# Collecting the states of a selective scan four units at a time instead of three

## The chip, the cores and the metric

The kernel runs on one NeuronCore of a Trainium2 chip. The metric is the device time of one execution in microseconds (us). Before the change it is 14725.35 us, the median of three runs (14713.78 to 14727.14). Engines are called as in the profile: PE is the matrix engine (PEld its weight loads), DVE the vector engine, ACT the scalar engine, POOL the GpSimd engine, SP the engine whose queue issues almost all DMAs.

## The reference

Four images of 96 channels and 64 x 64 points (L = 4096 points) pass through four layers: an attention layer, a two-dimensional selective scan with a convolutional block behind it (L1), a sharpening convolution (L2), and a second selective-scan layer (L3). The scan is what matters here. For each image it runs in four directions (rows and columns, forward and back) over 192 channels, each with 16 states:

```
h = h * exp(d * A) + (d * u) * B          # 16 states of every channel, point after point
y = sum over the 16 states of h * C       # one number per channel and point
Y = y_rows + y_rows_back + y_cols + y_cols_back + u * D
```

The sum over the 16 states in the second line is the part that the change regroups.

## The kernel before

**Units.** The eight scans (two layers, four images) make eight stages of 384 units, 3072 units in all. A unit is 8 channels x 16 states = 128 partitions, over a chunk of CH = 1024 points. Twelve units (NG) are a group: 96 channels (one half h of the 192), one direction, one chunk. There are 256 groups. The order of instructions in the loop is written out by hand, in `unit` (line 2036). For unit i it issues, in this order:

- on SP, `fetch(i+4)` (line 1936): the step sizes d of the unit's 8 channels are read from DRAM and repeated for 16 states, into one of 10 buffers `rep`; then the store of a finished y chunk, if there is one, and DMAs that were put off (`later`);
- on ACT, `decays(i+2)` (line 1943, shown in the profile at L1948): exp(d A), in place in `rep`;
- on DVE, `scan(i)` (L1969): the recurrence, into `hs`; then on ACT `carry_on` (L1977), which keeps the last state;
- on POOL, `times_c(i)` (L1981): hs * C, written back into the unit's `rep` buffer;
- on PE, where due, `collect(j)` (line 1983, PE instructions are all at L948): the sum over 16 states, as matmuls of `rep` with a 0/1 matrix `addn`, accumulated in the PSUM tile `acc`;
- on PE, `drive(i+2)` (line 1950): (d u) spread from `parts` over the 128 partitions into one of two PSUM tiles `bx`; it needs the buffer that `scan(i)` has read;
- on DVE, `times_b(i+1)` (L1962): bx * B, in place.

**Collecting three at a time.** PE can be split into column tiles of 32 columns, each with its own weights and its own moving operand. `place` (line 1930) hands out the channels so that three units in a row belong to three different column tiles: unit m of the group holds channels of column tile m % 3. A collect takes three units and is due when (i - 4) is a multiple of 3. One group has four collects; in the first, `acc` is started (and the chunk of y that a backward direction adds to is loaded into `yo`), after the last `output` (line 2000) writes `yo` from rows 0 to 95 of `acc`, and a DMA (L2017) stores it to a y image in DRAM. There is one `yo` buffer and one `acc`.

**Work beside the scan.** The other layers are generators (`first`, `second`, `third`, `last`, with `directions` and `finish` in them). Each `yield` hands control back to the scan loop. In stages 0, 3 and 4 the attention layer and its convolutions (`first`) of another image run beside the scan, in stages 1, 2, 5 and 6 the block behind the L1 scan (`second`), in stage 7 the rest of L3 for all four images. How much of it is issued in a unit is set by a budget, counted in matmuls:

```
PACE = {"first": 3.5, "second": 3.7, "third": 3.2}
owed = min(owed, 0.5) + PACE[...] - (2.1 if i % 3 == 1 else 0.0)
```

so a unit with a collect gives the work beside it 2.1 less. At most two pieces go into one unit. What is left of it 19 units before a stage's end is issued at once. `prepare(g)` (line 1835), also beside the scan, makes d, B, C and d u of the group after next.

**y images.** `directions` (line 1418) begins `second` and `third`: once the scan's last chunks are stored, it loads the row and column images of y for both halves h, in chunks of 96 x 1024 (L1430 and L1432), 8 DMAs for each half, with SP in between waiting for the last store. `last` and `finish` load y images too.

## Time and profile before

| | |
|---|---|
| median of three runs | 14725.35 us |
| span of the profiled execution | 14698.9 us |
| what lies around the span (median less span) | 26.5 us |
| first scan begins, last scan begins | 690.3 us, 14567.0 us |
| 3072 scans, DVE (L1969) | 7156.4 us busy, about 2.33 us each |
| 3072 products with B, DVE (L1962) | 3723.6 us busy, 1.21 us each |
| 1024 collects on PE (`acc`) | 2586.7 us busy |
| bytes moved by DMA | 2644.27 MB |
| mean granted PE clock | 0.817 |

The execution's own time was not recorded apart from its span, so the difference to the median of the runs stands in for start and end. A matmul with float32 operands appears as two weight loads and two MATMUL records, so a collect of six matmuls is twelve records. The distance from one scan to the next, here called the pitch, is the loop's time per unit; it is read from the records of L1969. Divided over sixteenths of a stage (24 units) it runs like this, in us:

| sixteenth | 1 | 2 | 3 | 4 | 5 | 6 | 7 | 8 | 9 | 10 | 11 | 12 | 13 | 14 | 15 | 16 |
|---|---|---|---|---|---|---|---|---|---|---|---|---|---|---|---|---|
| stage 0 (`first`) | 4.75 | 5.02 | 4.88 | 4.94 | 4.97 | 4.72 | 4.66 | 4.85 | 4.14 | 4.08 | 3.87 | 3.82 | 4.08 | 4.31 | 3.98 | 3.92 |
| stage 1 (`second`) | 5.99 | 5.31 | 4.04 | 3.99 | 3.94 | 4.06 | 4.27 | 4.48 | 4.03 | 4.80 | 4.92 | 3.75 | 4.09 | 4.27 | 3.75 | 3.96 |
| stage 7 (`third`, `last`) | 5.70 | 5.90 | 4.51 | 4.23 | 6.52 | 5.75 | 4.93 | 4.23 | 6.57 | 6.05 | 5.21 | 4.66 | 5.09 | 5.36 | 5.24 | 5.10 |

A stage is 1671 to 1730 us long, stage 7 is 2036 us.

### The profile page before, as it was taken

Reading aid. Unit: us, or ns where it says so; the run is one execution under the profiler, and the core shown is the slowest. Engines: PE = TensorE matmul, PEld = TensorE weight load, DVE = VectorE, ACT = ScalarE, POOL = GpSimd, SP = SyncE. Lnnn points to the kernel's source line nnn. Section 1 sums busy time; section 2 is a strip of 40 time slices with the busy share of each in tenths; the row PEclk is TensorE's granted clock in tenths of the full one; section 3 lists DMA queues with packets and bytes.
Section 4 is the critical chain, followed back from the end, with each engine's and each line's share of the span. In section 5 each row is a group of like instructions: output and inputs, shape, how many; then the busy total and the mean of one; then the engine's idle time right before and its main releaser. Section 6 shows DMA issues by size and latency. Waiting matters only on the chain.

```text
span 14698.9 us, 128101 instructions
## 1 busy us (share of the span) xinstructions
PE 12296.5 (84%) x40802; PEld 3348.5 (23%) x40802; DVE 11654.4 (79%) x7509; ACT 8721.7 (59%) x12340; POOL 10204.0 (69%) x4634
## 2 busy tenths in 40 slices
PE   8888987988889796889868887897979888777767
PEld 2322221222223121222212222222212222111111
DVE  0477888888878888778887888788888888778776
ACT  3355565556756666554755556566755567666554
POOL 0166787777868778667776788687777777666564
PEclk9878887988879787778867887897979888677666
DMA  0266787787878778667876778687787878776674
GB/s 9 72 158 163 188 212 198 188 204 184 221 175 200 197 199 209 154 166 193 211 189 160 178 200 220 172 205 189 203 200 189 204 190 215 175 181 169 165 182 108
DMA packets 902735, 2644.27 MB, mean 180 GB/s; under 512 B 107104, under 2 KB 257216, under 8 KB 902048
## 3 DMA queue, kind: packets, MB, share of 16 engines
q1 hardware_dynamic: 901392, 2634.72, 71.8%
q8 instruction: 324, 5.31, 0.2%
q14 instruction: 363, 2.97, 0.1%
q10 hardware_dynamic: 656, 1.27, 0.0%
HBM read 2168.97 MB, written 466.62 MB: 179 GB/s over the span
## 4 chain that ended last, share of the span: by engine, by line
PE 50%; DVE 20%; ACT 10%; DMA 7%; issue 6%; POOL 5%; SPq 1%; DVEq 0%; POOLq 0%; ACTq 0%
PE one L948 33%; DVE hs L1969 14%; PE acc L948 9%; PE bx L948 6%; DVE bx L1962 5%; DMA rep<-dd 3%; PE held L948 3%; POOL rep L1981 2%; ACT rep L1948 2%; ACT L1948 1%; ACT ex L1287 1%; ACT L1890 1%; DMA xz<-gate 0%; ACT delta L1888 0%; POOL delta L1893 0%
## 5 line engine op out<-in xcount | busy, mean ns | idle before, releaser
L1981 POOL TENSOR_TENSOR rep<-hs,bc 128x1024 f32<-128x1024 f32 x3072 | 7224.5, 2357 | 3210.5 <-DVE hs L1969 2664.2
L1969 DVE TENSOR_TENSOR_SCAN hs<-rep,carry,bx 128x1024 f32<-128x1024 f32 x2304 | 5401.7, 2344 | 274.0 <-POOL rep L1981 14.8
L1962 DVE TENSOR_TENSOR bx<-bx,bc 128x1024 f32<-128x1024 f32 x3072 | 3723.6, 1212 | 1086.2 <-PE bx L948 1063.5
L1948 ACT ACTIVATE rep<-rep,l_decay 128x1024 f32<-128x1024 f32 x3072 | 3495.7, 1143 | 513.3 <-DMA rep<-dd 493.8
L948 PE MATMUL bx<-parts,spread 24*128 24x512 bf16 x6144 | 1412.7, 435 | 1662.7 <-DVE hs L1969 1608.8
L948 PE MATMUL acc<-rep,ct 128*32 128x512 f32 x12288 | 2586.7, 741 | 9.8 <-POOL rep L1981 9.1
L1969 DVE TENSOR_TENSOR_SCAN hs<-rep,bx 128x1024 f32<-128x1024 f32 x768 | 1754.7, 2285 | 123.3 <-ACT carry L1977 29.0
L948 PEld LDWEIGHTS <-spread 24*128 24x128 bf16 x6144 | 310.4, 93 | 4154.6 <-DVE hs L1969 2755.2
L948 PE MATMUL one<-band,dg 96*96 96x512 f32 x2304 | 1075.9, 605 | 0.0
L948 PE MATMUL one<-upad,diag 96*96 96x512 f32 x2016 | 996.4, 632 | 0.0
L948 PE MATMUL one<-qq,kk 96*128 96x512 f32 x1152 | 818.8, 800 | 134.6 <-ACT ex L1287 84.0
L948 PEld LDWEIGHTS acc<-rep,ct 128*32 128x32 f32 x12288 | 506.2, 127 | 1742.4 <-issue 1494.2
L1287 ACT ACTIVATE ex<-one 128x512 f32<-128x512 f32 x576 | 343.1, 596 | 747.7 <-PE one L948 743.0
L948 PE MATMUL one<-pr,ct 6*96 6x512 f32 x1024 | 652.7, 728 | 84.3 <-DVE V L1192 10.4
L1948 ACT ACT_TABLE_LOAD x495 | 635.1, 1283 | 76.6 <-DMA rep<-dd 68.5
L948 PE MATMUL one<-hp,diag 96*96 96x512 f32 x1152 | 607.1, 668 | 28.6 <-POOL diag L1112 28.6
L948 PE MATMUL one<-vpad,diag 96*96 96x512 f32 x1200 | 611.7, 647 | 0.0
L1977 ACT COPY carry<-hs 128x1 f32<-128x1 f32 x2304 | 409.2, 178 | 308.4 <-DVE hs L1969 306.5
L948 PE MATMUL held<-ex,cols 128*32 128x256 f32 x3072 | 567.9, 450 | 7.9 <-ACT ex L1287 1.9
L948 PE MATMUL held<-ex,vT 128*32 128x256 f32 x3072 | 568.3, 451 | 0.0
L948 PEld LDWEIGHTS one<-band,dg 96*96 96x96 f32 x2304 | 346.6, 162 | 535.3 <-issue 516.8
L948 PEld LDWEIGHTS one<-upad,diag 96*96 96x96 f32 x2016 | 314.7, 169 | 489.2 <-issue 478.3
(3420 smaller groups left out, 14369.3 us busy)
## 6 DMA issues: line engine op xcount, KB each, us to landing
rep<-dd SPq DMA_DIRECT2D x3072, 512.0 KB
parts<-du SPq DMA_DIRECT2D x1024, 144.0 KB
bc<-rows SPq DMA_DIRECT2D x256, 512.0 KB
dd<-delta SPq DMA_DIRECT2D x256, 384.0 KB
du<-cut SPq DMA_DIRECT2D x256, 384.0 KB
us<-urow SPq DMA_DIRECT2D x128, 384.0 KB
du<-cut SPq DMA_DIRECT2D x256, 192.0 KB
yrow<-yo SPq DMA_DIRECT2D x128, 384.0 KB
```

What stands on the lines that cost most here:

```text
L948: nc.tensor.matmul(o, lhsT=lhsT, rhs=rhs, start=first, stop=last)
L1287: nc.scalar.activation(last.rearrange("p a b -> p (a b)"), p, AF.Exp, scale=HD**-0.5)
L1890: nc.scalar.activation(w, w, AF.Ln)
L1948: nc.scalar.activation(a, a, AF.Exp, scale=decay[tag][:, k, NG * h + m : NG * h + m + 1])
L1962: nc.vector.tensor_mul(bx, bx, ready[i // NG][2][:, 0, :])
L1969: nc.vector.tensor_tensor_scan(out=hs, data0=a, data1=bx, initial=carry[:, h, m : m + 1] if c else 0.0, op0=ALU.mult, op1=ALU.add)
L1977: nc.scalar.copy(carry[:, h, m : m + 1], live[i][1][:, CH - 1 : CH])
L1981: nc.gpsimd.tensor_tensor(a, hs, ready[i // NG][2][:, 1, :], ALU.mult)
```

## The change

Units are handed out over four column tiles in place of three, so that a collect takes four units and a group has three collects. Each column tile then holds 24 channels in 32 rows; rows 24 to 31 of each are zero. `acc` and `yo` and the y images in DRAM have 128 rows with these gaps. Whoever loads a y image into a tile of 96 rows does it in four DMAs of 24 rows (`ungapped`) where it was one of 96; the first chunk of an L3 row scan likewise loads u into `yo` in four. `yo` becomes one tile that lives through the kernel and is cleared once. The sums of D come from a new constant of 128 rows. There are 12 buffers `rep` in place of 10, and the space that the framework sets aside for descriptors of DMAs issued by POOL is cut to 1024 bytes (this kernel issues none there). The budget takes 2.1 off in every fourth unit, where it was every third. The collect follows its last unit at the same distance as before (`i - 5` with four units, `i - 4` with three), and the output comes in the same unit of the group.

```
-            dsum[tag] = derived(2)
-            nc.vector.tensor_reduce(dsum[tag], wv(tag + "d"), AX.X, ALU.add)
+            dsum[tag] = keep.tile([128, 2], F32, name=tag + "dsum")
+            nc.vector.tensor_reduce(dsum[tag], cv("d")[:, 0 if tag == "l1_" else 1], AX.X, ALU.add)
...
+    y_row, y_col = ([image(f"{k}{h}_", 128) for h in range(2)] for k in ("yrow", "ycol"))
+
+    def ungapped(dst, src, cols):
+
+        for q in range(4):
+            nc.sync.dma_start(out=dst[24 * q : 24 * q + 24], in_=src[32 * q : 32 * q + 24, cols])
...
                 for j in range(4):
-                    nc.sync.dma_start(out=t.rearrange("p a b -> p (a b)")[:, bass.ts(j, CH)],
-                                      in_=y_col[h][b][:, bass.ts(j, CH)])
-                    nc.sync.dma_start(out=V[:, h, bass.ts(j, CH)], in_=y_row[h][b][:, bass.ts(j, CH)])
+                    ungapped(t.rearrange("p a b -> p (a b)")[:, bass.ts(j, CH)], y_col[h][b], bass.ts(j, CH))
+                    ungapped(V[:, h, bass.ts(j, CH)], y_row[h][b], bass.ts(j, CH))
...
-        return g, m % 3 * 4 + m // 3
+        return g, m % 4 * 3 + m // 4
...
-        rep = sp.tile([128, CH], F32, name="rep", bufs=10)
+        rep = sp.tile([128, CH], F32, name="rep", bufs=12)
...
-        hs = [live.pop(i + q)[0] for q in range(3)]
-        w = addn[:, 24 - 8 * (m // 3) : 56 - 8 * (m // 3)]
+        hs = [live.pop(i + q)[0] for q in range(4)]
+        w = addn[:, 24 - 8 * (m // 4) : 56 - 8 * (m // 4)]
         for e in range(2):
-            for q in range(3):
-                mm(live["acc"][bass.ts(q, 32), bass.ts(e, PCH)], w, hs[q][:, bass.ts(e, PCH)], m == 0, m == NG - 3)
+            for q in range(4):
+                mm(live["acc"][bass.ts(q, 32), bass.ts(e, PCH)], w, hs[q][:, bass.ts(e, PCH)], m == 0, m == NG - 4)
...
-        j = i - BEHIND - 2
-        due = j >= 0 and j % 3 == 0
+        j = i - BEHIND - 3
+        due = j >= 0 and j % 4 == 0
...
-            owed = min(owed, 0.5) + PACE[BESIDE[s][0][0]] - (2.1 if i % 3 == 1 else 0.0)
+            owed = min(owed, 0.5) + PACE[BESIDE[s][0][0]] - (2.1 if i % 4 == 1 else 0.0)
...
-    nc = bacc.Bacc("TRN2", target_bir_lowering=False, num_devices=1)
+    nc = bacc.Bacc("TRN2", target_bir_lowering=False, num_devices=1,
+                   dynamic_dma_scratch_size=1024)
```

More of the change, by code (lines that the diff above doesn't have):

```diff
@@ L172, in _constants @@
     c["dtw2"] = s.reshape(128, 4, E)
+    s = np.zeros((4, 32, 2, 2, 4), np.float32)
+    for t, w in enumerate((i["L1_conv_Ds"], i["L3_conv_ss_D"])):
+        s[:, :24, t] = w.reshape(4, 2, 4, 24).transpose(2, 3, 1, 0)
+    c["d"] = s.reshape(128, 2, 2, 4)
     for tag, w in (("l1_", i["L1_conv_A_log"]), ("l3_", i["L3_conv_ss_Alog"])):
@@ L1024, in streams, with image @@
             nc.vector.tensor_scalar(decay[tag], src, -1.0, None, ALU.mult)
-            dsum[tag] = derived(2)
-            nc.vector.tensor_reduce(dsum[tag], wv(tag + "d"), AX.X, ALU.add)
-    def image(name):
-        return [dram.tile([96, L], F32, name=f"{name}{b}") for b in range(B)]
+            dsum[tag] = keep.tile([128, 2], F32, name=tag + "dsum")
+            nc.vector.tensor_reduce(dsum[tag], cv("d")[:, 0 if tag == "l1_" else 1], AX.X, ALU.add)
+    def image(name, rows=96):
+        return [dram.tile([rows, L], F32, name=f"{name}{b}") for b in range(B)]
     res1, res2, gate1, skip3, gate3 = (image(k) for k in ("res1_", "res2_", "gate1_", "skip3_", "gate3_"))
-    u_row, u_col, y_row, y_col = ([image(f"{k}{h}_") for h in range(2)] for k in ("urow", "ucol", "yrow", "ycol"))
+    u_row, u_col = ([image(f"{k}{h}_") for h in range(2)] for k in ("urow", "ucol"))
+    y_row, y_col = ([image(f"{k}{h}_", 128) for h in range(2)] for k in ("yrow", "ycol"))
+    def ungapped(dst, src, cols):
+        for q in range(4):
+            nc.sync.dma_start(out=dst[24 * q : 24 * q + 24], in_=src[32 * q : 32 * q + 24, cols])
     def group_norm(src, dst):
@@ L1643, in last @@
                     for j in range(4):
-                        nc.sync.dma_start(out=t.rearrange("p a b -> p (a b)")[:, bass.ts(j, CH)],
-                                          in_=y_col[h][b][:, bass.ts(j, CH)])
+                        ungapped(t.rearrange("p a b -> p (a b)")[:, bass.ts(j, CH)], y_col[h][b], bass.ts(j, CH))
                     yield 1
@@ L1683, in load @@
                     t = pool.tile([96, PCH], F32, tag=name, name=name, bufs=bufs)
-                    nc.sync.dma_start(out=t, in_=src[b][:, bass.ts(j, PCH)])
+                    if src[b].shape[0] == 128:
+                        ungapped(t, src[b], bass.ts(j, PCH))
+                    else:
+                        nc.sync.dma_start(out=t, in_=src[b][:, bass.ts(j, PCH)])
                     return t
@@ L1811, in streams @@
     carry = keep.tile([128, 2, NG], F32, name="carry")
+    yo = keep.tile([128, CH], F32, name="yo")
+    nc.gpsimd.memset(yo, 0.0)
     sums = keep.tile([96, len(SCANS), 4, 2, 2 * NCH], F32, name="sums")
@@ L1988, in collect @@
             live["acc"] = ps.tile([128, CH], F32, tag="acc", name="acc", bufs=1)
-            live["yo"] = sp.tile([96, CH], F32, name="yo", bufs=1)
             if back:
-                nc.sync.dma_start(out=live["yo"], in_=(y_row if axis == "r" else y_col)[h][b][:, natural(c, back)])
+                nc.sync.dma_start(out=yo, in_=(y_row if axis == "r" else y_col)[h][b][:, natural(c, back)])
             elif axis == "r" and tag == "l3_":
-                nc.sync.dma_start(out=live["yo"], in_=u_row[h][b][:, natural(c, back)])
-        hs = [live.pop(i + q)[0] for q in range(3)]
-        w = addn[:, 24 - 8 * (m // 3) : 56 - 8 * (m // 3)]
+                for q in range(4):
+                    nc.sync.dma_start(out=yo[32 * q : 32 * q + 24],
+                                      in_=u_row[h][b][24 * q : 24 * q + 24, natural(c, back)])
+        hs = [live.pop(i + q)[0] for q in range(4)]
+        w = addn[:, 24 - 8 * (m // 4) : 56 - 8 * (m // 4)]
         for e in range(2):
-            for q in range(3):
-                mm(live["acc"][bass.ts(q, 32), bass.ts(e, PCH)], w, hs[q][:, bass.ts(e, PCH)], m == 0, m == NG - 3)
+            for q in range(4):
+                mm(live["acc"][bass.ts(q, 32), bass.ts(e, PCH)], w, hs[q][:, bass.ts(e, PCH)], m == 0, m == NG - 4)
     def output(i):
@@ L2004, in output @@
         dst = (y_row if axis == "r" else y_col)[h][b][:, natural(c, back)]
-        yo = live["yo"]
-        ya = time(live["acc"][:96], back, 0, CH)
+        ya = time(live["acc"], back, 0, CH)
         if back:
@@ L2065, in unit @@
             times_b(i + 1)
-        if due and j % NG == NG - 3:
+        if due and j % NG == NG - 4:
             store.append(output(j))
@@ L2142, in streams @@
                 work.run()
-            owed = min(owed, 0.5) + PACE[BESIDE[s][0][0]] - (2.1 if i % 3 == 1 else 0.0)
+            owed = min(owed, 0.5) + PACE[BESIDE[s][0][0]] - (2.1 if i % 4 == 1 else 0.0)
             owed = unit(i, prep, work, owed)
-        for j in range(total - 3, total, 3):
+        for j in range(total - 4, total, 4):
             collect(j)
```

## The prediction

> **What bounds the kernel now.** I read the page's busy times first, then the pitch over sixteenths of a stage, then three windows, and last who makes DVE wait.

> ```profile
> PE 12296.5 (84%) x40802; PEld 3348.5 (23%) x40802; DVE 11654.4 (79%) x7509; ACT 8721.7 (59%) x12340; POOL 10204.0 (69%) x4634
> ...
> L948 PE MATMUL acc<-rep,ct 128*32 128x512 f32 x12288 | 2586.7, 741 | 9.8 <-POOL rep L1981 9.1
> ```

> PE is busiest, but no engine is full. The windows say why (columns: us, busy PE, PEld, DVE, ACT, POOL, then PE clock, DMA share, GB/s). First attention in stage 0, second the convolutions of stage 1, third the end of stage 0, where nothing but scan and `prepare` is left:

> ```profile
> 1116.00:1329.00 213.00, 192.13 (x919) 48.43 (x918) 159.24 (x97) 119.16 (x184) 143.35 (x63) 0.79 0.67 167
> 2664.00:2950.00 286.00, 285.62 (x918) 86.68 (x916) 251.22 (x145) 176.58 (x252) 234.38 (x102) 0.99 0.80 198
> 2299.00:2393.00 94.00, 46.14 (x160) 8.28 (x160) 85.32 (x51) 48.79 (x53) 77.97 (x35) 0.61 0.89 216
> ```

> In the convolutions PE is full at full clock (285.62 of 286), with a pitch of 4.0 us. In attention it is 90% busy at clock 0.79 and waits on exponentials in between; pitch 4.9. Where no work is beside the scan, DVE is 91% busy, and the pitch, 3.9, comes close to scan and product (2.33 + 1.21 = 3.54). So a stage is a stretch at PE's pace and a tail at DVE's. The waits of DVE agree: the scan loop's large wait is for PE's `drive`.

> ```profile
> DVE bx L1962 <- PE bx L948: 1063.5, 485, 27.1
> ...
> DVE yo L2008 <- PE acc L948: 190.6, 84, 9.2
> ```

> At each start of `second` there is a third regime, where SP's queue decides. In order of time, stage 1:

> ```profile
> 2408.72 2.29 DVE L1969 TENSOR_TENSOR_SCAN hs<-rep,bx 128x1024 f32<-128x1024 f32 x1
> ...
> 2411.30 0.31 SPq L1430 DMA_DIRECT2D yc<-ycol  x1
> 2411.66 0.42 SPq L1432 DMA_DIRECT2D V<-yrow  x1
> ...
> 2415.51 0.52 SPq L1940 DMA_DIRECT2D rep<-dd  x1
> ...
> 2429.72 1.15 ACT L1948 ACTIVATE rep<-rep,l_decay 128x1024 f32<-128x1024 f32 x1 [3.87 <-DMA rep<-dd]
> ```

> Eight y loads of 384 KB go out in 4.2 us, and the `rep` fetch behind them lands 18.4 us after the first. The scans around it start at 2412.26, 2422.85 and 2431.04: about 12 us lost.

> [...] the three tiles of a collect start within 14 ns of each other, at 2402.393, and the next three 0.852 us later, what one untiled matmul part takes at the same half clock; attention already runs four such tiles side by side at the same rate. [...] The trace's clock records are only 0.5 and 1.0; hence a collect of 1.85 us at full clock and 3.16 us or more at half. [...]

> **The change part by part.**

> *Collects.* 1024 become 768; a collect of four tiles should take what one of three takes. The mean is 2586.7 / 1024 = 2.53 us, so PE is freed of 256 x 2.53 = 647 us. Beside work it is less, at a higher clock: 31.59 us for 14 collects in the attention window (2.26 each), 46.83 for 24 in the convolutions (1.95). Per unit a collect costs 0.75 and 0.65 us there, and would cost 0.56 and 0.49: 0.19 and 0.16 freed, say 0.18.

> *Budget.* It rises from 3.5 - 0.7 = 2.8 to 3.5 - 0.525 = 2.975 in `first`. So PE's freed time is filled with more work per unit, and that work ends earlier. I took the end from the two programs' instruction orders: the last PE instruction beside the scan falls in unit 353 before and 335 after (stages 0, 3, 4), 349 and 331 (stages 1, 2, 5, 6). In each of seven stages 18 units move from the busy stretch (pitch about 4.4 over 350 units) to the tail (3.9). With n busy units, side work S, other cost c per busy unit on the path and tail pitch f, a stage takes S + n c + (384 - n) f. The gain is 18 (c - f) + 333 x (what of 0.18 is on the path). If PE is the whole path, S / n is about 2.8 and c 1.6: 18 x (1.6 - 3.9) + 333 x 0.18 = -41 + 60 = 19 us. If none of it is on the path, neither is S; then only the pitch counts: 18 x (4.4 - 3.9) = 9 us. I take 13, for seven stages 91. The bad end is a collect hidden while S is not: -41 per stage.

> *Stage 7.* 128 collects become 96. The chain there gives `acc` 7.0% of 2036 us, 142 us; a quarter is 36 us. Its tail of 132 us after the last scan hardly changes, and the last image's blocks wait for stored chunks either way. I take 30 (0 to 45).

> *y loads in four.* SP issues 64 loads at a stage start where it issued 16, at 0.38 to 0.47 us each (parts loads of 24 rows have a median of 376 ns), so 32 take at least 12 us against 4.2. In the program, a DMA also waits until the one eight before it on SP has landed. 3 MB at the 228 GB/s that the packets show in this burst is 13.8 us[...]. The fetch then comes behind seven small loads, not 3 MB, so it lands some 3 us later than before: 14 bursts x 3 = 42 us, with what is queued behind (d, u, parts). Range 0 (issue stays ahead of the bytes) to 130 (9 us each).

> *Bytes.* 256 stores and 128 backward loads grow by 128 KB: 50 MB, 1.9% of 2644 MB, 220 us of DMA time over the run. DMA share is 0.75 to 0.79 in the stages, 0.89 in the tails, so little shows: 10 us (0 to 40).

> *12 buffers.* A fetch may go when the unit 12 before is collected: 7 to 10 units earlier against 6 to 8. SP's own waits at L1940 for PE are 1843.3 + 1533.0 us, and ACT waits 493.8 us for `rep`; on the chain it is 3%, 441 us. But the y store of each group holds SP until DVE's output (L2017 waits 2419 us in all), so the lead is often lost again. Gain 25 us (0 to 120).

> *At nothing:* output on 128 partitions (free size sets its 1.21 us), `yo` cleared once, the constant, the four u loads (32 chunks, issued eight units ahead), the POOL space. `acc` and `yo` are reused one unit later than before, a little easier. Without that cover the u loads would cost 3 x 0.4 us x 32 = 38 us.

> Sum: -91 - 30 + 42 + 10 - 25 = -94. Span 14698.9 - 94 = 14605, plus 26.5 around it: 14632 us, 0.6% less.

> **Rivals.**

> *Bursts of small loads stall the scan (slower).* Place: SP at the 14 starts. If the eight-in-flight rule makes every eight loads wait a full landing (8.05 to 14.19 us is what the chain shows for a `rep` fetch), a burst of 32 takes 4 x 8 = 32 us, not 18: +14 x 14 = 196 in place of 42, hence 14785. It decides from 42 + 94 = 136, that is 10 us a burst. For it: the scan already stalls there. Against: 96 KB lands faster than 512.

> *Nothing gained.* The freed PE time is eaten by heavier units, the 13 per stage are near 0: 14723. For it: PE is full exactly where budget refills it; with S on the path, 41 / 60 = 68% of the freed 0.18 must be on it too, to break even.

> *Fetches run ahead.* The deeper ring frees the scan of most late `rep`: 100 more, and 19 per stage: 14490. Against: DVE's scan waits little behind ACT's decay directly.

> *Four tiles do not run side by side:* a collect costs a third more, PE gains nothing, the heavier units remain: 7 x 41 = 287 slower, with loads, bytes and buffers 314, so 15040. Attention's four tiles speak against it.

> **How the numbers follow.** Forecast 0.50 (14560 to 14700); fetches run ahead 0.09; nothing gained 0.17; bursts stall, or a like loss on SP, 0.22; tiles not parallel 0.02. A measurement tells about 0.2%, 29 us, from no change. Forecast's few near the edge go to "same": faster 0.57, same 0.19, slower 0.24. The range 14500 to 14800 leaves out about a tenth on each side.

> **What would show it.** `acc`: still 12288 records, but in 768 collects, about 1940 us busy. The last two sixteenths of stages 0 to 6 at 3.8 to 3.9, those before within 0.1 of the old pitch. In a start burst, the gap from the first y load to the next fetch's landing: 18 to 23 us. ACT's wait for `rep` below 490. The prediction is wrong if the busy pitch rises by more than 0.25, or the burst gap passes 28 us.

## The result and the profile after

The changed kernel takes 15035.1 us (median; 15023.8 to 15049.23), the kernel before on the same chip 14719.57 us (14692.79 to 14727.14): a ratio of 1.0222, 95% interval 1.0208 to 1.0237. It is slower by 2.2%, some 327 us by this ratio (the medians lie 315.5 us apart), where 0.6% less was forecast. The profiled execution has a span of 15047.4 us against 14698.9, 348.5 us more.

The page's busy times and the group of the collects, in the kernel after (lines have moved: PE L953, `times_b` L1976, `decays` L1962, `scan` L1983, `fetch` L1954):

```profile
PE 12147.7 (81%) x40802; PEld 3315.9 (22%) x40802; DVE 11688.5 (78%) x7509; ACT 8710.3 (58%) x12333; POOL 10200.1 (68%) x4635
...
L953 PE MATMUL acc<-rep,ct 128*32 128x512 f32 x12288 | 2087.7, 802 | 10.2 <-POOL rep L1995 10.2
```

The collects are 499.0 us less busy (2586.7 to 2087.7), and four tiles do run side by side: the four matmuls of a round start within 20 ns (2810.478 to 2810.498). Yet PE as a whole is only 148.8 us less busy, and it idles 497 us longer (span less busy time, 2899.7 against 2402.4). The mean granted clock fell from 0.817 to 0.784. The clock records are 0.5 or 1.0; added up, PE was at half clock for 6496 us against 5382.

The same three windows as before (us, busy PE, PEld, DVE, ACT, POOL, clock, DMA share, GB/s): attention in stage 0, convolutions of stage 1, end of stage 0.

```profile
1047.00:1302.00 255.00, 226.16 (x1051) 55.58 (x1051) 177.19 (x107) 136.02 (x197) 157.25 (x69) 0.75 0.62 152
2737.00:3027.00 290.00, 286.96 (x950) 88.94 (x949) 252.61 (x145) 180.37 (x258) 234.46 (x103) 1.00 0.82 199
2268.00:2357.00 89.00, 45.03 (x160) 8.90 (x160) 85.58 (x52) 54.97 (x80) 78.47 (x35) 0.55 0.97 256
```

In this stretch of the convolutions nothing is lost, and nothing gained: it was at full clock before, too. In attention the clock is 0.75 where it was 0.79, and the pitch of the scan is 5.30, 5.30, 5.33 and 4.99 us in sixteenths 3 to 6 of stage 0 (4.88, 4.94, 4.97, 4.72 before). The tail is a little faster, 3.69 and 3.79 (3.98 and 3.92), but 18 units longer, so it now fills both last sixteenths.

Who waits, after:

```profile
DVE bx L1976 <- PE bx L953: 1147.4, 566, 27.3
ACT rep L1962 <- DMA rep<-dd: 651.6, 310, 12.6
SPq L1930 <- ACT cut L1924: 1481.5, 206, 16.4
SPq L1954 <- PE bx L953: 674.0, 327, 19.0
```

DVE waits 84 us more for PE's `drive`, although PE has less to do. SP's large waits at `fetch` for PE (1843.3 and 1533.0 us before) shrank to 491.9 and 674.0 us, as 12 buffers allow. But SP's wait for `cut` at `prepare`'s load (L1930) was 248.3 us before, and ACT waits for `rep` longer than before (493.8 us).

The start of stage 1, in order of time:

```profile
2471.69 2.29 DVE L1983 TENSOR_TENSOR_SCAN hs<-rep,bx 128x1024 f32<-128x1024 f32 x1 [0.95 <-ACT carry L1991]
2472.86 1.53 SPq L1044 DMA_DIRECT2D yc<-ycol  x4
...
2480.70 2.29 DVE L1983 TENSOR_TENSOR_SCAN hs<-rep,bx 128x1024 f32<-128x1024 f32 x1
...
2486.99 2.09 SPq L1044 DMA_DIRECT2D V<-yrow  x4
2489.32 0.52 SPq L1954 DMA_DIRECT2D rep<-dd  x1
...
2495.39 1.15 ACT L1962 ACTIVATE rep<-rep,l_decay 128x1024 f32<-128x1024 f32 x1 [9.91 <-DMA rep<-dd]
```

Thirty-two small loads hold SP for 16.2 us; the fetch behind them lands 22.5 us after the first (18.4 before).

To see where the 350 us lie, I divided the stages into their sixteenths and took, for each part, its length, the union of PE's records, and the time at half clock, after less before:

| part | length | PE busy | PE idle | at half clock |
|---|---|---|---|---|
| stages 0, 3, 4: sixteenths 1 to 8 (attention, and the units behind it) | +142 | +118 | +24 | +235 |
| the same: 9 to 14 | +39 | -7 | +46 | +63 |
| the same: 15 and 16 (tail) | -31 | -118 | +87 | +193 |
| stages 1, 2, 5, 6: 1 and 2 (start) | +84 | +52 | +32 | +195 |
| the same: 3 to 14 | +65 | -40 | +105 | +94 |
| the same: 15 and 16 | -24 | -120 | +96 | +190 |
| stage 7 | +77 | -32 | +109 | +145 |

The first row is not attention alone. From the start of each stage to the end of attention's last matmul (the last one into `held`), the three stages take 2642 us after and 2649 before. But that matmul falls in unit 171 where it fell in unit 180, so this row has 27 more units of the scan behind attention. Up to there PE has 51 collects fewer and is only 25 us less busy; it is at half clock for 158 us more, worth up to 79 us of full clock (matmuls of 96 x 512 follow each other at 0.43 us at full clock, at 0.85 at half, medians in the kernel before). These are the two stretches of stage 0, before and after:

```profile
690.34:1571.63 881.29, 743.27 (x3423) 208.88 (x3423) 669.84 (x407) 521.27 (x810) 603.55 (x274) 0.77 0.68 167
```

```profile
689.57:1566.97 877.40, 728.84 (x3355) 203.21 (x3355) 639.13 (x388) 502.76 (x791) 573.79 (x261) 0.75 0.66 160
```

So attention takes the same time with fewer collects, and fewer units of the scan pass under it.

### The profile page after: what moved, and what is told of

It reads as the page before. It is cut to its first block, busy times and chain, and to the rows that moved or that the text cites. A ratio compares the mean times of both kernels' runs of the same rounds, so it can differ in the third digit from the quotient of the medians.

```text
span 15047.4 us, 128181 instructions
## 1 busy us (share of the span) xinstructions
PE 12147.7 (81%) x40802; PEld 3315.9 (22%) x40802; DVE 11688.5 (78%) x7509; ACT 8710.3 (58%) x12333; POOL 10200.1 (68%) x4635
## 2 busy tenths in 40 slices
DMA packets 920400, 2694.64 MB, mean 179 GB/s; under 512 B 112480, under 2 KB 262592, under 8 KB 919712
## 4 chain that ended last, share of the span: by engine, by line
PE 40%; DVE 16%; ACT 9%; DMA 6%; issue 4%; POOL 3%; SPq 1%; DVEq 0%; POOLq 0%; ACTq 0%
PE one L953 28%; DVE hs L1983 11%; PE acc L953 6%; PE bx L953 4%; DVE bx L1976 4%; DMA rep<-dd 3%; ACT rep L1962 2%; PE held L953 2%; POOL rep L1995 2%; ACT L1962 1%; DMA yc<-ycol 1%; ACT L1904 1%; ACT ex L1298 0%; ACT delta L1902 0%; DMA du<-cut 0%
## 5 line engine op out<-in xcount | busy, mean ns | idle before, releaser
L1983 DVE TENSOR_TENSOR_SCAN hs<-rep,carry,bx 128x1024 f32<-128x1024 f32 x2304 | 5402.9, 2345 | 272.4 <-POOL rep L1995 20.0
L1976 DVE TENSOR_TENSOR bx<-bx,bc 128x1024 f32<-128x1024 f32 x3072 | 3729.2, 1214 | 1167.6 <-PE bx L953 1147.4
L1962 ACT ACTIVATE rep<-rep,l_decay 128x1024 f32<-128x1024 f32 x3072 | 3494.8, 1143 | 666.6 <-DMA rep<-dd 651.6
L953 PE MATMUL bx<-parts,spread 24*128 24x512 bf16 x6144 | 1481.4, 457 | 2079.2 <-DVE hs L1983 2014.3
L953 PE MATMUL acc<-rep,ct 128*32 128x512 f32 x12288 | 2087.7, 802 | 10.2 <-POOL rep L1995 10.2
L1983 DVE TENSOR_TENSOR_SCAN hs<-rep,bx 128x1024 f32<-128x1024 f32 x768 | 1755.1, 2285 | 187.4 <-ACT carry L1991 81.5
L953 PEld LDWEIGHTS <-spread 24*128 24x128 bf16 x6144 | 314.0, 94 | 4715.1 <-DVE hs L1983 3104.4
L953 PE MATMUL one<-band,dg 96*96 96x512 f32 x2304 | 1092.2, 611 | 0.0
L953 PE MATMUL one<-upad,diag 96*96 96x512 f32 x2016 | 1000.4, 635 | 7.7 <-ACT upad L1158 5.5
L953 PE MATMUL one<-qq,kk 96*128 96x512 f32 x1152 | 828.9, 808 | 137.3 <-ACT ex L1298 96.0
L953 PE MATMUL one<-pr,ct 6*96 6x512 f32 x1024 | 784.3, 868 | 55.6 <-DVE V L1203 9.6
L953 PEld LDWEIGHTS acc<-rep,ct 128*32 128x32 f32 x12288 | 409.7, 133 | 1445.0 <-issue 1285.1
L953 PE MATMUL one<-hp,diag 96*96 96x512 f32 x1152 | 585.0, 649 | 30.7 <-POOL diag L1123 30.7
L953 PE MATMUL one<-vpad,diag 96*96 96x512 f32 x1200 | 609.8, 647 | 0.0
L953 PE MATMUL held<-ex,cols 128*32 128x256 f32 x3072 | 576.1, 456 | 8.5 <-ACT ex L1298 1.9
L953 PE MATMUL held<-ex,vT 128*32 128x256 f32 x3072 | 576.4, 456 | 0.0
L953 PEld LDWEIGHTS one<-band,dg 96*96 96x96 f32 x2304 | 350.9, 164 | 531.0 <-issue 526.9
L953 PEld LDWEIGHTS one<-upad,diag 96*96 96x96 f32 x2016 | 316.4, 170 | 494.1 <-issue 474.8
```

Of the source, the lines that this page charges most:

```text
L953: nc.tensor.matmul(o, lhsT=lhsT, rhs=rhs, start=first, stop=last)
L1962: nc.scalar.activation(a, a, AF.Exp, scale=decay[tag][:, k, NG * h + m : NG * h + m + 1])
L1976: nc.vector.tensor_mul(bx, bx, ready[i // NG][2][:, 0, :])
L1983: nc.vector.tensor_tensor_scan(out=hs, data0=a, data1=bx, initial=carry[:, h, m : m + 1] if c else 0.0, op0=ALU.mult, op1=ALU.add)
```

## Experiments

All ratios are to the kernel before on the same chip, with 95% intervals; "clock" is the mean granted clock and "half" the time at half clock in the profiled execution (before: 0.817 and 5382 us).

### What the collects alone are worth

Run e4 is the kernel before without the second of the four collects of a group, so that its sums lack three units of twelve. Nothing else is changed, neither budget nor loads.

```
-        for e in range(2):
+        for e in range(0 if m == 3 else 2):
```

> The kernel before with the second of the four collects of every group left out (its 6 matmuls; the sums then lack three units of twelve). PE is freed of 256 collects, 647 us busy, exactly what the change frees; budget, loads and buffers stay. Prediction's term (0.18 us of every busy unit is on the path): 7 x 333 x 0.18 + 36 = 450 us less, 14270. Rival (work beside the scan goes at its own pace, and PE's clock falls when PE has less to do): 14600 to 14720, with a lower mean clock than 0.817.

Measured: 1.0173 (1.0156 to 1.019), clock 0.774, half 6767 us. Leaving out a quarter of PE's collect work costs about 255 us, more than either expectation had; the clock fell, as the second had it. By the same division into sixteenths, 171 us lie in sixteenths 3 to 14 of stages 1, 2, 5, 6 (half clock +604), 79 in 9 to 14 of stages 0, 3, 4, and sixteenths 1 to 8 of these are 27 us shorter. This is not where the changed kernel loses most: there the budget refills the freed time.

Run e9 is the same kernel with the six matmuls put back as dead weight: zeros as weights, a constant tile as the moving operand. The `rep` buffers come free as in the run above.

```
+                if m == 3:
+                    mm(live["acc"][...], nothing, ready[g][2][:, 0, bass.ts(e, PCH)], False, False)
+                else:
```

> The kernel before, whose second of four collects per group issues its six matmuls with a weight of zeros and a constant operand, so PE keeps its work while that collect's three units are missing from the sums (the result lacks them); the rep buffers come free as in the run that left those matmuls out. Theory of the clock (a unit without a collect lets PE idle, the granted clock falls, and everything on PE takes longer): PE's work is back, so clock 0.81 to 0.82 and 14650 to 14760 us, at the time of the kernel before. Rival of the buffers and fetches (what slowed the run without those matmuls is that rep buffers come free at other times and fetches collide): still 14900 to 15000 us.

Measured: 1.0002 (0.9995 to 1.001), clock 0.818, half 5362 us. So the loss in e4 is due to PE's missing work, not to buffers or fetches. The window of stage 1's band convolutions, from first to last matmul, 118 units in both; first without the collects:

```profile
2674.40:3165.60 491.20, 478.40 (x1393) 145.57 (x1392) 417.47 (x241) 287.29 (x421) 386.57 (x170) 0.94 0.77 190
```

and with the zeros in their place:

```profile
2632.20:3104.40 472.20, 469.05 (x1514) 143.03 (x1512) 417.09 (x241) 288.03 (x422) 387.63 (x170) 0.99 0.81 198
```

With 121 fewer records PE is busy 9.4 us longer, and idle 12.8 us in place of 3.2. Half clock covers 58 us of the first window and 7 of the second. PE's records inside the first window show one such stretch:

```profile
2873.15 3.67 PE L948 MATMUL one<-band,dg 96*96 96x512 f32 x8
...
2878.38 1.09 PE L948 MATMUL one<-pr,ct 6*96 6x512 f32 x2
2880.96 0.39 PE L948 MATMUL bx<-parts,spread 24*128 24x512 bf16 x2 [1.49 <-DVE hs L1969]
...
2887.42 6.52 PE L948 MATMUL one<-band,dg 96*96 96x512 f32 x8
2893.86 1.92 PE L948 MATMUL acc<-rep,ct 128*32 128x512 f32 x12
```

In a unit without a collect, PE comes to its `drive` before the scan has left the `bx` buffer, and waits 1.49 us. From 2882.93 to 2893.17, for 10.24 us, the clock is at half, and eight band matmuls take 6.52 us where they took 3.67. In the records from 2869.73 us on, the 1.49 us are the only idle time over 0.15 us ahead of the drop. This is a single gap; that it brought the drop about is not shown. Over the whole run of e4 against e9, half clock is 1405 us longer; PE is 98 us busier though it has 1536 matmuls fewer, and it idles 183 us more. So slower matmuls used up more than all the time that the collects left free, and longer waits come on top.

### Budget and the end of the side work

Run e2: the kernel before with the changed kernel's higher budget (3.5 - 1.575 / 3 = 2.975), all collects kept; the side work ends in units 313 and 331:

```
-(2.1 if i % 3 == 1 else 0.0)
+(1.575 if i % 3 == 1 else 0.0)
```

> The kernel before with 1.575 in place of 2.1 taken off in every third unit: the mean budget is the changed kernel's, collects stay as they were. Work beside the scan ends at unit 313 (stages 0, 3, 4) and 331 (1, 2, 5, 6): 40 and 18 units earlier. Theory A: slower, by 3 x 40 + 4 x 18 = 192 units at 3.8 us less what the busy units gain; if the busy stretch keeps its length in us, up to 700 us, I expect 15000 to 15300. Theory B: within 60 us of before.

Measured: 1.0141 (1.0124 to 1.0158), clock 0.816, between the two expectations. A higher budget by itself costs some 207 us, with the mean clock as before: side work that is packed tighter shortens the busy stretch by less than the tail grows.

Run e1: the kernel after with the budget of before on the mean (2.8 in place of 2.1; ends in 341 and 353):

> The changed kernel with 2.8 taken off the budget in every fourth unit where it takes 2.1, so that the mean budget is what it was before (2.8 in stages 0, 3, 4). By the instruction order the work beside the scan then ends at unit 341 (stages 0, 3, 4) and 353 (1, 2, 5, 6), against 335 and 331 in the changed kernel and 353 and 349 before. Theory A (the raised budget pushes work beside the scan into fewer units at the pace of that work itself, so every freed unit is paid at the tail's 3.75 us): 22 units x 4 and 6 x 3 units move back under cover, some 100 x 3 us, about 300 us less at most, I expect 14800 to 14900. Theory B (the bursts of small y loads are the loss): within 50 us of the changed kernel's 15035.

Measured: 1.0204 (1.0183 to 1.0225), which can't be told from the kernel after (1.0208 to 1.0237), as theory B had it. Run e13, with the end of the last side work itself put back, by pace rather than by deduction (352 and 349; 353 and 349 before):

```
-    PACE = {"first": 3.5, "second": 3.7, "third": 3.2}
+    PACE = {"first": 3.15, "second": 3.52, "third": 3.2}
```

> The kernel after with side work let in at 3.15 and 3.52 a unit in place of 3.5 and 3.7, so that it ends in unit 352 and 349 of a stage, where it ends in the kernel before (353 and 349), in place of 335 and 331. Theory of the end (18 units a stage moved to the tail are the loss, about 2 us each): at least 200 us of the 315 lost come back, 14780 to 14850 us. Theory of the clock (PE with less work per unit idles and falls to half clock): less work per unit, so the clock stays at 0.78 or falls, and 14920 to 15000 us.

Measured: 1.0150 (1.0133 to 1.0167), clock 0.788: 0.72%, 106 us, come back, a third of the loss; between the two expectations. Attention's own end is not put back by this: it still falls in unit 171. Run e14: the kernel before with a still later end (3.35 and 3.55; units 361 and 359):

> The kernel before with side work let in at 3.35 and 3.55 a unit in place of 3.5 and 3.7, so that it ends in unit 361 and 359 in place of 353 and 349. Theory of the end (a unit moved from the tail into the busy stretch saves 1 us or more): 7 stages x 9 units x 1 us, 14610 to 14660 us. Theory of the clock (less side work per unit, more idle PE): no gain, 14690 to 14800 us with the clock at 0.80 to 0.815.

Measured: 0.9986 (0.9978 to 0.9993), clock 0.817: about 20 us faster than the kernel before, the only kernel that beats it, and by less than the 0.2% that a measurement tells here. The gain per unit that the first theory took is too large by a factor of three.

### The small loads

Run e3: the kernel before with its y loads in four DMAs of 24 rows:

> The kernel before with each 96-row load of a y image issued as four loads of 24 rows, and nothing else. The first 28 units of a stage and the 4 ahead took 183 us before and 201 to 210 us after the change at the start of stages 1, 2, 5, 6, 177 and 194 at the start of stage 7. Theory B: this brings those 95 + 17 us and about 20 more at the two later bursts of stage 7: 14850 (14810 to 14890). Theory A: the bursts are a small part, below 14760.

Measured: 1.0040 (1.0025 to 1.0054), clock 0.818, 59 us, just under theory A's bound. Run e7: the changed kernel with images of 96 rows (whole loads, but stores and backward loads of `yo` in four):

```
-        for q in range(4):
-            nc.sync.dma_start(out=dst[24 * q : 24 * q + 24], in_=src[32 * q : 32 * q + 24, cols])
+        nc.sync.dma_start(out=dst, in_=src[:, cols])
```

> The changed kernel with y images of 96 rows again: y is stored in four DMAs of 24 rows (one group in 12 units) and loaded in one; backward chunks are loaded into yo in four. The bursts at stage starts are then as before. From what loads in four cost the kernel before (58 us): 14975, with the first 28 units of stages 1, 2, 5, 6 and the 4 ahead back near 183 us. If the bursts only add to waits that are there anyway, above 15010.

Measured: 1.0196 (1.0179 to 1.0213), clock 0.786: 0.26% or 38 us less than the kernel after, about an eighth of the loss. The intervals of the two kernels overlap a little, and e7 has its stores and backward loads in four. The starts of stages 1, 2, 5, 6 take 193 to 201 us in it, not the 183 expected, so the loads are only a part of what these starts lose.

### Three attempts to raise the clock, none of which gained

Zero matmuls, four rounds a group, added ahead of the matmuls of two collects, where they delay the `drive`: in the kernel after (e5), in the kernel before (e6), and in the kernel after without gaps (e8).

> The changed kernel with PE work that has no effect added to the second and third collect of each group: four of its matmuls again with weights of zero, into acc. That is four rounds of column-tile matmuls per group, as much PE time as the change took away (a quarter of the collects of before). Theory C (a collect is PE's densest work; with fewer of them the granted clock falls, and that slows all PE work): time at half clock falls from 6496 us to 5300 to 5700, mean clock back to 0.81 or more, and the kernel gets faster although PE does more: 14740 to 14850. Rival (freed PE time was on the path, only budget and loads cost): 15035 plus 100 to 450 us.

> The kernel before with the same kind of empty matmuls added to the second and fourth collect of each group (four rounds per group, 25% more collect work). Theory C: if the slope of the clock continues, mean clock 0.83 to 0.86 and 14500 to 14690; if it saturates, within 50 us of before. Rival: 0.18 us more per busy unit on the path, 450 us slower, 15150.

> Both: images without gaps and empty matmuls. If clock and bursts are separate causes they add: e5 less 58 us, about 14730, with what is left over the kernel before due to the raised budget (0 to 60 us).

Measured: 1.0369 (1.0352 to 1.0386), 1.0154 (1.0137 to 1.0171) and 1.0331 (1.0314 to 1.0348). The clock rose each time (0.784 to 0.804, 0.817 to 0.831, 0.786 to 0.807), the time by about 200 us. In e6, 96 us of it lie in sixteenths 3 to 14 of stages 1, 2, 5, 6, where PE was 90% busy before. The likely reading is that filling lies on the path where PE is nearly full. Only e5 fell where an expectation had it, the rival's. A higher mean clock is thus no aim in itself.

Halves: the matmuls of the first 512 columns in one unit, those of the second 512 in the next, with 1.05 off the budget in both; in the kernel after (e10, shown), in the kernel before (e11) and in the kernel after without gaps (e12).

```
-        for e in range(2):
-            for q in range(4):
-                mm(live["acc"][bass.ts(q, 32), bass.ts(e, PCH)], w, ...)
+        for q in range(4):
+            mm(live["acc"][bass.ts(q, 32), bass.ts(e, PCH)], w, ...)
...
+            collect(j, 0)
+        if late:
+            collect(j - 1, 1)
```

> The kernel after with each collect in two halves: the four matmuls of the first 512 columns in one unit, those of the second 512 in the next; the budget is lowered by 1.05 in both units instead of 2.1 in one. Same work on PE in all, but two units of four have PE work of the collect instead of one. Theory of the clock (what costs is units in which PE runs out of work): clock above 0.79 and 14850 to 14970 us. Rival (the clock is a symptom; what costs is the side work's place alone, which is unchanged on the mean): 15000 to 15070 us.

> The kernel before with each collect in two halves of three matmuls, in two units of three instead of one, the budget lowered by 1.05 in both. Theory of the clock: clock above 0.82 and 14550 to 14680 us, faster than both kernels. Rival (place of the collect's work is of no account): 14680 to 14740 us.

> The kernel after with images of 96 rows in DRAM (stores and backward loads in four, y loads whole) and the collects in halves. Both causes taken together: clock theory and load theory give 14800 to 14930 us; if the halves do nothing, 14997 us as without them.

Measured: 1.0339 (1.0315 to 1.0362), 1.0048 (1.0031 to 1.0065) and 1.0325 (1.0307 to 1.0343), with a clock of 0.768, 0.811 and 0.773, lower than without halves (0.784, 0.817, 0.786). Both theories missed. The halves also change the rhythm of the budget: with no unit starved, attention takes two pieces in every unit, and the products of its queries and keys are through after 114 units, where before took 131. In the kernel before that shortened this part of stage 0 from 631.6 to 549.5 us at a clock of 0.91, but it also ends 23 units earlier, and the run as a whole gained nothing. Run e15 adds a slower pace that moves the end to units 359 and 366:

> The kernel before with the collects in halves, and side work let in at 2.95 and 3.45 a unit, so that it ends in units 359 and 366. If the halves gain once their side work doesn't end early: 14550 to 14690 us. If they only move attention's work into fewer units, and a longer tail was not what cost: 14750 to 14850 us.

Measured: 1.0051 (1.0034 to 1.0068), clock 0.815. No gain either; putting the end back brought nothing here.

### What is left when loads and end are undone

Run e16: the kernel after without gaps and with the pace 3.15 and 3.52:

> The kernel after with images of 96 rows in DRAM and y loads whole, and the side work's end put back to units 352 and 349 as in e13. Theories of the end and of the loads together: 14740 to 14800 us. Clock theory: 14880 to 14960 us, since the sum of the collects' PE work is still a quarter less; what it lacks to 14710 is then the clock's share.

Measured: 1.0106 (1.0083 to 1.0128), clock 0.792, half 6178 us, just under the clock theory's times. Half of the loss is gone, 156 us stay. By the same division, against before: sixteenths 1 to 8 of stages 0, 3, 4 +134 us (half clock +225), starts of stages 1, 2, 5, 6 +54 (+180), stage 7 +43 (+120), and sixteenths 3 to 14 of stages 1, 2, 5, 6 -48. Attention in the three stages takes 2644 us (2649 before) and still ends in unit 171, so the +134 are again the 27 units behind it. In stages 1, 2, 5, 6 the gain in sixteenths 3 to 14 makes up for the loss at the starts.

In run e17 PE's missing quarter is put back as zeros in a unit of its own, with 2.1 off the budget there and the original pace (ends in 353 and 349):

```
+        elif j >= 0 and j % NG == 6:
+            for e in range(2):
+                for q in range(4):
+                    mm(live["acc"][...], nothing, ready[i // NG][2][:, 0, bass.ts(e, PCH)], False, False)
```

> The kernel after with images of 96 rows in DRAM and y loads whole, and with eight more matmuls of zero weight on a constant operand in one unit of twelve, between the second and the third collect of a group, for which the budget is lowered by 2.1 as for a collect. PE then has as much work as in the kernel before, and the side work ends in units 353 and 349, as there. Theory of the clock and the end: clock 0.81 to 0.82 and 14650 to 14760 us, all that is lost comes back. Rival (four units at a time have another cost: sums later, buffers, larger outputs): 14850 us or more.

Measured: 1.0151 (1.0124 to 1.0178), clock 0.806, half 5779 us. The clock theory, in the form "what PE lacks is work", falls here: with as much work, the same end and whole loads it is still 220 us slower than before, in the rival's range. Attention ends in unit 180 again, and up to there the three stages take 2715 us against 2649, with 1393 us at half clock against 1230. Stage 0, units 48 to 120, in the kernel before, in e16 and in e17, one line each:

```profile
924.00:1279.00 355.00, 318.88 (x1532) 81.00 (x1530) 260.41 (x155) 204.23 (x302) 235.27 (x102) 0.80 0.65 159
```

```profile
928.00:1300.00 372.00, 328.26 (x1580) 81.45 (x1580) 264.42 (x157) 205.62 (x307) 235.65 (x103) 0.78 0.64 152
```

```profile
927.00:1293.00 366.00, 334.60 (x1630) 83.22 (x1626) 261.73 (x155) 203.54 (x303) 235.22 (x103) 0.76 0.64 154
```

e16 has 440 `held` matmuls of each kind in these 72 units, the other two 420 each. In e17 PE idles less than before (31.4 against 36.1 us) and still has the lower clock. So neither the amount of work nor the amount of idling decides it. What differs on PE is the order: before has a collect in every third unit; in e17 collects and zeros follow each other at 4, 2, 2 and 4 units. That this rhythm is the cause is argued, not shown. The kernel of e17 also has 12 `rep` buffers, sums of 128 rows, and stores and backward loads in four, and no run takes these back one by one.

Run e18: the same zeros in the kernel after as it is, with its small loads:

> The same zero collect in the kernel after, with its gapped images and its y loads, u loads and stores as they are. What it takes above e17 is the price of the small loads and larger transfers: 40 to 65 us by the earlier runs, 14690 to 14820 us. If the loads only cost where the clock is low, it equals e17.

Measured: 1.0206 (1.0178 to 1.0234). The loads and gaps cost 79 us here, more than expected. Together with e3 (59), e7 (38) and e16 against e13 (65), they cost 38 to 79 us.

## Why the prediction was wrong

**The step that failed is the sum under "Budget"**, 18 (c - f) + 333 x (what of 0.18 is on the path), with the result of 13 us gained a stage. Its second term took all freed PE time as a gain or, at worst, as nothing. Run e4, which leaves a quarter of the collects out of the kernel before, has this term alone, and there it is a loss of about 255 us. The step held the granted clock of each regime fixed while it took work from PE; half clock rose by 1114 us in the changed kernel instead. In attention one sees the result: 51 collects fewer, some 115 us at the prediction's 2.26 us each, took 6 us off the time to its end. I had the clock of 0.79 in attention in a shown line, and used it only to price a collect. A collect itself takes 1.92 us at full clock and 3.63 at half (medians), not 1.85 and 3.16.

The second case of the sum, 9 us, also held the busy pitch fixed while more side work went into each busy unit. The same attention in nine units fewer is a longer pitch, 4.9 us a unit before and 5.15 after (2649 us over 540 units, 2642 over 513).

The first term was too large for each unit moved. It has 2.3 us; with the higher budget alone (e2) stages 0 to 6 are 142 us longer for 192 units moved, 0.74 each. (Stage 7 is 85 us longer there.) I named "the bad end", -41 a stage, and gave it no chance of its own. Stages 0 to 6 did become 275 us longer, 39 each, but with the small loads in it, so that the nearness is in part luck.

Of the 327 us, by subtraction of runs, the earlier end of the last side work accounts for 106 and the small loads for 65; 156 remain. They are not the clock's alone: in e16's profile, 171 us longer than before, 130 lie in stages 0, 3 and 4, where attention still ends nine units early, and 43 in stage 7. How they divide is not shown. The single runs don't add up either: e4, e2 and e3 cost 255, 207 and 59 us, 521 in all.

**Stage 7** was taken at -30 and became 77 us longer (2036 to 2114 us). Its time at half clock rose by 145 us, but PE also idles 109 us more there, loads in four alone lengthen it by 34 us (e3) and the budget alone by 85 (e2). How the 77 divide stays open. The 7.0% of the prediction was read over the first half of the stage; over all of it `acc` has 7.5% of the chain.

**y loads in four** were sized about rightly: +42 predicted, 38 to 79 measured. The time from the first load to the landing of the fetch is 22.5 us (18 to 23 predicted). The rival with full landings, 196 us, did not happen: 32 loads went out in 16.2 us, with SP waiting at 18 of them (5.1 us in all) until the load eight before had landed. The loads so waited for took 3.4 to 4.8 us from issue to landing, not the 8.05 or more of a fetch.

**12 buffers** were taken at -25 us. ACT's wait for `rep` should have fallen below 490 us and rose to 651.6. SP's two waits for PE at the fetch fell from 3376 to 1166 us, and its wait for `cut` at L1930 rose from 248 to 1482. No run has the buffers alone, so their share in time stays open.

**Tiles in parallel** was right: a collect at full clock has a median of 1.92 us with three tiles and with four. Attention's four start within 20 ns in the kernel before, the next four 0.24 us after them at full clock (256 columns; a collect's rounds of 512 are 0.45 apart). (The start given for the three tiles, 2402.393, is 5002.393 in the trace.) The rival without it happens to name 15040 us, close to what came, by a mechanism that the trace refutes.

**Output on 128 rows** takes no longer: a median of 1.220 us (128 x 1024), where 96 x 1024 took 1.217 before; DVE's tensor-tensor instructions of 96 x 512 took 0.677.

**Bytes** came as counted (2694.64 MB, +50.4); their share in time can't be told from that of the loads.

**The signs named** for a wrong prediction: the busy pitch rose by 0.36 in sixteenths 3 to 8 of stage 0 (mean 4.84 to 5.19), over the 0.25 named; the collects were 2087.7 us busy, not 1940; the tail pitch, 3.68 to 3.86, came out at or a little under the 3.8 to 3.9 named.

**What stays open.** Why e17 gets a lower clock in attention than the kernel before, at equal work and less idling, and whether another spacing of three collects would keep it. Where PE is 90% busy, in sixteenths 3 to 14 of stages 1, 2, 5, 6, fewer collects were a loss of 171 us with nothing in their place (e4) and a gain of 48 with the budget refilling them at the slower pace (e16); no run takes that apart.

## What to carry to other kernels

Where an engine's granted clock falls when work is taken from it, as here (0.817 to 0.774 in e4), removed work is not time gained: look for the stretches in which it already idles and count half-clock time there before pricing the saving. If a budget refills the freed time, price what the refill moves elsewhere, here 18 units a stage into a tail at 3.8 us each, and nine from under attention. Test such a change by leaving the work out, and by putting it back as zeros at the same place, before building what it needs.
